# Seven block products planned by the whole PSUM bank in two phases, and other margins for choosing DVE

## The chip, the cores and the metric

The kernel runs on one core of a Trainium2 chip. The metric is the device time of one execution in microseconds, the median of several runs. The span of a profiled execution, from its first to its last instruction, is some 2 us (1.7 to 2.2) shorter than the time of the same execution. All runs told of here are in the fast state (granted TensorE clock 0.995 to 1.0). Runs of one call share a chip, and different calls may have had different chips: the kernel before had medians of 1513.98, 1514.43, 1515.01, 1515.30 and 1514.85 us in the five calls.

## The reference, cut to what matters

The input is 64 graphs of 256 nodes with 128 features, and one adjacency matrix `adj` (256 x 256) for all. Four graph layers follow one another; the change is in the first, a gated recurrence of five steps whose first product is with the adjacency matrix.

```python
def step(h, _):                                   # layer 0, five times
    m_in  = jnp.einsum('nm,bmd->bnd', in_matrix, h)    # in_matrix = out_matrix = adj
    m_out = jnp.einsum('nm,bmd->bnd', out_matrix, h)
    av = jnp.concatenate([m_in, m_out], axis=-1)
    u3 = h @ u3_w.T + u3_b
    z  = jax.nn.sigmoid(av @ w3_w.T + w3_b + u3)
    r  = jax.nn.sigmoid(av @ w4_w.T + w4_b + u3)
    hv = jnp.tanh(av @ w5_w.T + w5_b + (r * h @ u5_w.T + u5_b))
    h  = (1.0 - z) * h + z * hv
    ...                                            # layers 1 to 3 and the norms: cut
```

## The kernel before

The kernel treats two graphs at a time (32 pairs). It does not write its instructions in the order of the program text. A planner (`Schedule`) collects operations with the values that each reads and writes, the engines that could do it and a time for each, then lays them out one by one at the earliest start, and so fixes the order on every engine before the kernel runs. The parts that matter:

```python
SPARE = {"DVE": 0.6, "DVE+": 1.0, "POOL": 0.4}    # added to an option's end when an engine is chosen
MARGIN, LAG = 1.06, 0.8                           # LAG: margin between an operation and who waits for it
...
for engine, us, fn in op.ways:                    # choice of the engine (cut)
    start = max(op.ready, held, *(engines[e] for e in USES.get(engine, (engine,))))
    end = start + us + SPARE.get(engine, 0.0)
```

"DVE+" is a DVE operation with two SBUF operands, which the planner keeps apart from Pool's (both need what it calls PORT). The product with the adjacency matrix is done as seven 128x128 block products in place of eight (a Winograd form) in the five steps of 28 of the 32 pairs, so 140 times. They accumulate in three column parts (blocks of 128 columns) of one PSUM bank, and between them the partial sums are read out:

```python
def spread7(h, right, terms):
    sv, t, o = Value("A", name="sums"), Value("PS", name="ps"), Value("A", name="mT")
    X, Y, V = (Part(t) for _ in range(3))         # to the planner: three independent values
    ...
    product(0, H(0, 0), B(0, 0), [h], [X, Y, V], start=True)
    sum_(...)  sum_(...)  sum_(...)               # s1|s3, s2, s4: DVE or Pool
    copy(0, 0, [X], [o0])                         # ScalarE or DVE, 128 columns
    product(1, s1, T(0), [p1, V], [V])
    copy(3, 1, [V], [o3])
    product(2, H(0, 1), B(1, 0), [h, Y], [Y])
    plus(0, 2, [Y, o0], [o, o0])                  # DVE: PSUM + SBUF
    product(0, s2, T(1), [p2, X], [X])
    copy(1, 0, [X], [o1])
    product(1, s4, B(1, 1), [p4, V], [V])
    plus(1, 1, [V, o1], [o, o1])
    product(0, s3, T(2), [p1, X], [X])
    plus(3, 0, [X, o3], [o, o3])
    product(0, H(1, 1), T(3), [h, X], [X])
    copy(2, 0, [X], [o])
    return o
```

## Time and profile before

| | before |
|---|---|
| time, median (runs) | 1513.98 us (1513.24 to 1515.22, 4 runs) |
| TensorE, DVE, ScalarE, Pool busy | 99%, 79%, 66%, 41% |
| matmul records | 7156, of which 1960 are block products (line 565) |

TensorE is the engine to look at, and 99% is nearly all. But a busy TensorE in the profile includes modelled ends, which hide up to 0.17 us of every pause (two records of 128 columns are shown 0.39 us long and take 0.22 in a dense stream). So for this document I counted **gaps**. A gap is the distance from one matmul's start to the next, less what the first one takes in a dense stream (111.3 ns for 128 columns, 215.8 for 256, 429.2 for 512, as the traces show; 113.5 was taken for 130, where they show 111.8, which is 0.4 us in the whole sum; two records for each fp32 matmul), wherever that is over 25 ns. The dense stream is 1485.2 us long in both kernels. In the kernel before the gaps sum to 20.7 us, and 12.8 of them lie ahead of block products (L565 of the kernel before, the line of the helper that issues them). For the steady middle part of the span, 400 to 1300 us, they sum to 9.5 us. The windows view shows that part more coarsely; its columns are TensorE, weight loads, DVE, ScalarE and Pool busy, then clock, DMA share and GB/s:

```profile
400.00:1300.00 900.00, 895.51 (x4287) 628.89 (x4286) 724.28 (x1848) 606.30 (x1914) 393.53 (x515) 1.00 0.70 147
```

TensorE is without work for 4.5 us of 900 here; the other half of the 9.5 us is under modelled ends.

### The profile page before, as it was taken

What the parts mean: (1) busy time and instruction counts of PE and PEld (TensorE: products, weight loads), DVE (VectorE), ACT (ScalarE), POOL (GpSimd) and SP (SyncE); (2) the same over time, 40 slices, a digit from 0 to 9 for tenths busy, and PEclk for the clock granted to TensorE, in tenths of its full rate; (3) what the DMA queues carried; (4) which work ended last, traced back from release to release, by engine and by line L of the source; (5) the groups of instructions that cost most, each with busy time, mean ns of one, the idle gap of its engine ahead of it and who ended that gap; (6) DMA issues with size and microseconds to landing.
All of it is one profiled execution on the core that took longest, in us unless ns stands there. A gap on an engine that the chain in (4) does not pass through costs nothing.

```text
span 1513.6 us, 26330 instructions
## 1 busy us (share of the span) xinstructions
PE 1498.1 (99%) x7156; PEld 1060.8 (70%) x7156; DVE 1191.8 (79%) x3102; ACT 1006.1 (66%) x3173; POOL 626.9 (41%) x835
## 2 busy tenths in 40 slices
PE   9999999999999999999999999999999999999998
PEld 7556566767776677667676677676676666788987
DVE  7865778898889887888788878667878778789861
ACT  3444456787777676677666676665677567778974
POOL 5212233545455453445543454243444233335552
PEclk9999999999999999999999999999999999999999
DMA  6544456887888686677575776576676577678453
GB/s 195 131 82 93 98 127 137 166 174 161 171 177 171 130 163 152 135 152 163 125 162 125 157 166 132 124 153 134 128 159 133 122 157 156 124 164 173 96 120 77
DMA packets 936515, 214.39 MB, mean 142 GB/s; under 512 B 717744, under 2 KB 931888, under 8 KB 936368
## 3 DMA queue, kind: packets, MB, share of 16 engines
q1 hardware_dynamic: 936368, 212.71, 66.7%
q8 instruction: 58, 0.95, 0.3%
q14 instruction: 89, 0.73, 0.2%
HBM read 115.81 MB, written 96.80 MB: 140 GB/s over the span
## 4 chain that ended last, share of the span: by engine, by line
PE 94%; DVE 3%; ACT 1%; DMA 1%; issue 1%; SPq 0%; POOLq 0%; ACTq 0%; POOL 0%; DVEq 0%
PE ps L565 14%; PE ps L545 13%; PE ps L705 9%; PE ps L706 9%; PE ps L698 9%; PE ps L690 9%; PE ps L691 9%; PE ps L727 7%; PE ps L841 4%; PE ps L834 3%; PE ps L797 3%; PE ps L833 3%; PE ps L757 2%; DVE b L772 1%; DVE a L576 0%
## 5 line engine op out<-in xcount | busy, mean ns | idle before, releaser
L565 PEld LDWEIGHTS ps<-aTt,a 128*128 128x128 f32 x1064 | 165.5, 191 | 82.5 <-issue 56.3
L579 POOL TENSOR_TENSOR a<-a 128x256 f32<-128x256 f32 x100 | 83.0, 830 | 296.8 <-DMA a<-e 102.7
L576 DVE TENSOR_TENSOR a<-ps,a 128x128 f32<-128x128 f32 x420 | 109.6, 280 | 106.0 <-PE ps L565 84.9
L565 PE MATMUL ps<-aTt,a 128*128 128x128 f32 x1064 | 186.6, 276 | 5.1 <-DVE a L576 3.9
L708 ACT ACTIVATE a<-ps,bzrh 128x512 f32<-128x512 f32 x160 | 109.9, 687 | 109.6 <-PE ps L706 104.4
L572 ACT COPY a<-ps 128x128 f32<-128x128 f32 x489 | 117.4, 272 | 88.9 <-PE ps L565 70.1
L694 ACT ACTIVATE a<-ps,bzrh 128x512 f32<-128x512 f32 x160 | 110.0, 690 | 91.5 <-PE ps L691 74.3
L705 PE MATMUL ps<-a,w 128*128 128x512 f32 x320 | 163.6, 593 | 0.0
L706 PE MATMUL ps<-a,u5h 128*128 128x512 f32 x320 | 163.4, 592 | 0.0
L691 PE MATMUL ps<-a,w 128*128 128x512 f32 x320 | 163.4, 592 | 0.0
L698 PE MATMUL ps<-a,w 128*128 128x512 f32 x320 | 162.2, 593 | 0.0
L526 DVE STREAM_TRANSPOSE a<-a 128x512 f32<-128x512 f32 x217 | 151.1, 700 | 10.8 <-PE ps L706 2.2
L727 PEld LDWEIGHTS ps<-W,a 128*128 128x128 f32 x1024 | 135.6, 192 | 33.0 <-issue 29.2
L651 ACT ACTIVATE a<-ps 128x128 f32<-128x128 f32 x456 | 121.1, 287 | 48.2 <-PE ps L727 23.8
L659 POOL TENSOR_TENSOR s<-s,neg_half 128x4 f32<-128x4 f32 x128 | 144.4, 1128 | 9.3
L235 ACT COPY a<-ps 128x512 f32<-128x512 f32 (+1 forms) x164 | 85.2, 523 | 88.8 <-PE ps L545 59.6
L700 ACT ACTIVATE a<-ps,bzrh 128x512 f32<-128x512 f32 x160 | 109.7, 689 | 51.1 <-PE ps L698 42.3
L727 PE MATMUL ps<-W,a 128*128 128x128 f32 x1024 | 141.8, 275 | 0.0
L690 PE MATMUL ps<-a,W 128*128 128x512 f32 x256 | 131.1, 594 | 0.7 <-DVE x L673 0.7
L656 POOL TENSOR_SCALAR s<-s 128x4 f32<-128x4 f32 x96 | 30.0, 313 | 239.3 <-ACT a L651 199.4
L565 PEld LDWEIGHTS ps<-aT,a 128*128 128x128 f32 x728 | 108.4, 191 | 26.4 <-issue 20.8
L565 PE MATMUL ps<-aT,a 128*128 128x128 f32 x728 | 125.7, 276 | 0.6 <-issue 0.2
(199 smaller groups left out, 3367.9 us busy)
## 6 DMA issues: line engine op xcount, KB each, us to landing
e<-a SPq DMA_DIRECT2D x279, 256.0 KB
a<-e SPq DMA_DIRECT2D x1116, 64.0 KB
e<-b SPq DMA_DIRECT2D x29, 512.0 KB
b<-e SPq DMA_DIRECT2D x116, 128.0 KB
x<-x_in SPq DMA_DIRECT2D x32, 256.0 KB
t<-xT_in SPq DMA_DIRECT2D x32, 256.0 KB
a<-d SPq DMA_DIRECT2D x32, 256.0 KB
y_out<-a SPq DMA_DIRECT2D x32, 256.0 KB
```

The lines of the kernel that those rows point to most:

```text
L526: dve(n / 512 * 0.55 + 0.09, lambda: nc.vector.transpose(st.at(n), i.at(n)), [i], [st])
L545: nc.tensor.matmul(t.at(2, N)[:, b, :], tokens(i)[:, 2 * b + j, :], right.ap[:, j, :], start=(b == j == 0), stop=(j == 1), skip_group_chec ...
L565: pe(mm(128), lambda: nc.tensor.matmul(blk(t, k), left(), rt(), start=start, stop=True, skip_group_check=True), [*r, right, terms], w)
L572: S.add([("ACT", 0.18, lambda: nc.scalar.copy(blk(o, to), blk(t, k))), ("DVE", 0.2, lambda: nc.vector.tensor_copy(blk(o, to), blk(t, k)))] ...
L651: nc.scalar.activation(tokens(junk)[:, c, :], v.at(len(tiles), D)[:, k, :], AF.Square, scale=D ** -0.5, accum_out=mv()[:, c, 1:2])
L659: pool(1.02, lambda: nc.gpsimd.tensor_tensor(rs(), rs(), neg_half.ap, op=ALU.pow), [s, neg_half], [s])
L690: nc.tensor.matmul(t.at(512), mat("u3"), hT.at(512), start=True, stop=False)
L691: nc.tensor.matmul(t.at(512), w4.ap, mT.at(512), start=False, stop=True)
L698: pe(mm(512), lambda t=t, mT=mT: nc.tensor.matmul(t.at(512), w3.ap, mT.at(512), start=False, stop=True, skip_group_check=True), [w3, mT, t ...
L705: nc.tensor.matmul(t.at(512), w5.ap, mT.at(512), start=True, stop=False)
L706: nc.tensor.matmul(t.at(512), u5h.ap, r.at(512), start=False, stop=True)
L727: nc.tensor.matmul(tokens(t)[:, c, :], tokens(i)[:, c, :], w(), start=(first and k == c == 0), stop=(k == len(lefts) - 1), skip_group_chec ...
```

## The change

Its intent, as its title says: seven block products in two phases of one PSUM bank, with more room for DVE, each hand-over planned later, and two-operand sums preferred on Pool. The diff does the first of these. Its two SPARE numbers go down, and so make DVE more attractive to the planner than before, so for them I went by the diff and not by the words.

```diff
-SPARE = {"DVE": 0.6, "DVE+": 1.0, "POOL": 0.4}
+SPARE = {"DVE": 0.3, "DVE+": 0.6, "POOL": 0.4}
@@ spread7
-        sv, t, o = Value("A", name="sums"), Value("PS", name="ps"), Value("A", name="mT")
+        sv, o, t = Value("A", name="sums"), Value("A", name="mT"), bank()
-        X, Y, V = (Part(t) for _ in range(3))
-        o0, o1, o3 = (Part(o) for _ in range(3))
-        def product(k, left, rt, r, w, start=False):
-               [*r, right, terms], w)
+        def product(k, left, rt, r, start=False):
+               [*r, right, terms, *[t] * (not start)], [t])     # the whole bank
 ...                                   (the three sums stay; the old products and copies go)
+        product(0, H(0, 0), B(0, 0), [h], start=True)
+        product(1, s1, T(0), [p1])
+        product(3, s3, T(2), [p1])
+        product(2, s2, T(1), [p2])
+        evacuate(lambda: o.at(512), lambda: t.at(512), [t], [o])
+        sum_(0.335, 0.8, ... o[0:2] + o[2:4] ..., [o], [p1])
+        product(0, H(0, 1), B(1, 0), [h])
+        product(3, H(1, 1), T(3), [h])
+        product(1, s4, B(1, 1), [p4])
+        sum_(0.2, 0.46, ... blk(o, 3) ..., [p1], [o])
+        evacuate(lambda: blk(o, 0), lambda: blk(t, 0), [t], [o], (0.17, 0.2))
+        dve(0.335, ... tensor_add(o[1:3], t[1::2], sv[0]) ..., [t, p1], [o])
```

More of the change, by code (lines that the diff above doesn't have):

```diff
@@ L550, in spread7 @@
     def spread7(h, right, terms):
-        sv, t, o = Value("A", name="sums"), Value("PS", name="ps"), Value("A", name="mT")
+        sv, o, t = Value("A", name="sums"), Value("A", name="mT"), bank()
         p1, p2, p4 = (Part(sv) for _ in range(3))
-        X, Y, V = (Part(t) for _ in range(3))
-        o0, o1, o3 = (Part(o) for _ in range(3))
-        blk = lambda v, k, n=1: v.at(512)[:, k * P:(k + n) * P]
+        blk = lambda v, k: v.at(512)[:, k * P:(k + 1) * P]
         H = lambda b, j: lambda: blk(h, 2 * b + j)
@@ L562, in spread7 @@
         s3, s1, s2, s4 = (lambda k=k: blk(sv, k) for k in range(4))
-        def product(k, left, rt, r, w, start=False):
+        def product(k, left, rt, r, start=False):
             pe(mm(128), lambda: nc.tensor.matmul(blk(t, k), left(), rt(), start=start, stop=True, skip_group_check=True),
-               [*r, right, terms], w)
+               [*r, right, terms, *[t] * (not start)], [t])
         def sum_(us, us_pool, fn, r, w):
             S.add([("DVE+", us, lambda: fn(nc.vector)), ("POOL", us_pool, lambda: fn(nc.gpsimd))], r, w)
-        def copy(to, k, r, w):
-            S.add([("ACT", 0.18, lambda: nc.scalar.copy(blk(o, to), blk(t, k))),
-                   ("DVE", 0.2, lambda: nc.vector.tensor_copy(blk(o, to), blk(t, k)))], r, w)
-        def plus(to, k, r, w):
-            dve(0.2, lambda: nc.vector.tensor_add(blk(o, to), blk(t, k), blk(o, to)), r, w)
-        product(0, H(0, 0), B(0, 0), [h], [X, Y, V], start=True)
         sum_(0.335, 0.8, lambda e: e.tensor_sub(sv.at(4, P)[:, 0:2], h.at(4, P)[:, 0::2], h.at(4, P)[:, 2:4]), [h], [p1])
@@ L581, in spread7 @@
         sum_(0.2, 0.46, lambda e: e.tensor_add(s4(), s2(), H(0, 1)()), [h, p2], [p4])
-        copy(0, 0, [X], [o0])
-        product(1, s1, T(0), [p1, V], [V])
-        copy(3, 1, [V], [o3])
-        product(2, H(0, 1), B(1, 0), [h, Y], [Y])
-        plus(0, 2, [Y, o0], [o, o0])
-        product(0, s2, T(1), [p2, X], [X])
-        copy(1, 0, [X], [o1])
-        product(1, s4, B(1, 1), [p4, V], [V])
-        plus(1, 1, [V, o1], [o, o1])
-        product(0, s3, T(2), [p1, X], [X])
-        plus(3, 0, [X, o3], [o, o3])
-        product(0, H(1, 1), T(3), [h, X], [X])
-        copy(2, 0, [X], [o])
+        product(0, H(0, 0), B(0, 0), [h], start=True)
[3 more added lines that the diff above has]
+        evacuate(lambda: o.at(512), lambda: t.at(512), [t], [o])
+        sum_(0.335, 0.8, lambda e: e.tensor_add(sv.at(4, P)[:, 0:2], o.at(4, P)[:, 0:2], o.at(4, P)[:, 2:4]), [o], [p1])
+        product(0, H(0, 1), B(1, 0), [h])
+        product(3, H(1, 1), T(3), [h])
+        product(1, s4, B(1, 1), [p4])
+        sum_(0.2, 0.46, lambda e: e.tensor_add(blk(o, 3), blk(sv, 0), blk(sv, 1)), [p1], [o])
+        evacuate(lambda: blk(o, 0), lambda: blk(t, 0), [t], [o], (0.17, 0.2))
+        dve(0.335, lambda: nc.vector.tensor_add(o.at(4, P)[:, 1:3], t.at(4, P)[:, 1::2],
+                                                blk(sv, 0)[:, None, :].to_broadcast([P, 2, P])), [t, p1], [o])
         return o
```

## The prediction

> **What bounds the kernel now.** I read the page first, then the waits of TensorE, then windows of 100 us, then single stretches of the timeline. The page's engine totals and its chain of waits:
>
> ```profile
> PE 1498.1 (99%) x7156; PEld 1060.8 (70%) x7156; DVE 1191.8 (79%) x3102; ACT 1006.1 (66%) x3173; POOL 626.9 (41%) x835
> ...
> PE 94%; DVE 3%; ACT 1%; DMA 1%; issue 1%; SPq 0%; POOLq 0%; ACTq 0%; POOL 0%; DVEq 0%
> ```
>
> TensorE is busy nearly throughout and carries 94% of the chain that ends last. No other engine is a bound on average. What TensorE waited for, in full:
>
> ```profile
> PE ps L565 <- DVE a L576: 3.9, 9, 1.2
> PE ps L295 <- DVE ones L293: 1.2, 1, 1.2
> PE ps L545 <- DMA a<-e: 1.2, 1, 1.2
> PE ps L565 <- ACT a L572: 1.0, 3, 0.6
> PE ps L690 <- DVE x L673: 0.7, 1, 0.7
> ```
>
> L565 is the helper that issues the seven block products, L572/L573 their copies out of PSUM, L576 the PSUM additions. So the changed part is the one that TensorE visibly waits in, but for 5 us of 1513.6 only.
>
> "Busy" uses modelled ends, so I also count starts. The groups by shape hold about 3,820 matmul records of 128 (or 130) columns, 1,720 of 256 and 1,600 of 512 (every fp32 product shows as two records). Inside a burst the timeline gives 0.111 us per 128-column record, 0.216 per 256 and 0.43 per 512:
>
> ```profile
> 508.22 0.61 PE L565 MATMUL ps<-aTt,a 128*128 128x128 f32 x4
> 508.66 0.61 PE L565 MATMUL ps<-aT,a 128*128 128x128 f32 x4
> 509.11 0.39 PE L565 MATMUL ps<-aTt,a 128*128 128x128 f32 x2
> 509.33 0.39 PE L565 MATMUL ps<-aT,a 128*128 128x128 f32 x2
> 509.55 0.60 PE L833 MATMUL ps<-vx,a 128*128 128x256 f32 x2
> 509.99 0.59 PE L834 MATMUL ps<-vq,a 128*128 128x256 f32 x2
> ```
>
> (508.22 to 508.66 is four records of 128, 509.55 to 509.99 two of 256.) The sum is 3820 x 0.111 + 1720 x 0.216 + 1600 x 0.43 = 424 + 372 + 688 = 1484 us. With 1.2 us before the first matmul and 6.1 after the last (1513.6 less 1507.5), the matmuls alone need 1491 us. **All the slack there is comes to about 22 us, 1.5% of the span**, and part of it is start-up and the last pairs, which the change does not touch.
>
> DVE is the second engine, and in places it is much closer to its limit than 79%:
>
> ```profile
> 300.00:400.00 100.00, 99.60 (x493) 69.90 (x492) 90.00 (x252) 78.97 (x264) 45.12 (x62) 1.00 0.81 170
> 400.00:500.00 100.00, 99.59 (x490) 70.90 (x489) 88.40 (x228) 71.10 (x225) 49.82 (x62) 1.00 0.82 171
> 500.00:600.00 100.00, 98.55 (x499) 71.36 (x498) 80.66 (x202) 66.54 (x222) 47.24 (x64) 1.00 0.70 144
> ```
>
> (columns: TensorE, weight loads, DVE, ACT, Pool busy). At DVE 90% TensorE still lost only 0.4 us of 100.
>
> [...] this is how the longest visible TensorE wait arose:
>
> ```profile
> 509.78 1.45 POOL L803 TENSOR_TENSOR a<-a,rbc 128x512 f32<-128x512 f32 x1
> ```
>
> ```profile
> 510.03 1.48 DVE L772 CUSTOM_DVE_ANT_0 b<-a,maskb 128x256 f32<-128x256 f32 x1
> ...
> 512.87 1.14 DVE L696 SCALAR_TENSOR_TENSOR a<-a,t 128x512 f32<-128x512 f32 x1
> 513.93 0.47 DVE L576 TENSOR_TENSOR a<-ps,a 128x128 f32<-128x128 f32 x2
> ```
>
> The L772 operation (median 0.42 us) took 1.48 until Pool's ended; another was stretched behind the next Pool sum; L576 came late, and the product at 514.55 waited 1.17 us for it.
>
> [...] Here the 128x256 sum (L579) has a median of 0.73 us on Pool and 0.416 on DVE, 1.76 times.
>
> [...] The kernel before orders a step's products and evacuations by column part of one bank; the kernel after orders them by the whole bank. No row of the trace before shows a collision or its cost, so I put no time on this.
>
> **The change part by part.** The block products are used in 28 of the 32 pairs, in 5 steps: 140 calls.
>
> TensorE: seven products before, seven after. Still 140 x 7 x 2 = 1960 records. No matmul time is removed.
>
> Hand-overs: before, block 0 of the bank is written, read and rewritten three times, so TensorE waits on an evacuation up to five times a call (V, Y, X parts). After, four products are issued, one evacuation follows, then three products: one hand-over. With the planner's own constants block 0's old chain is about four products (0.22+1.03 each, with its margin for the semaphore) and four reads (0.2+0.96): 9.6 us; the new one 4 products, a 0.5 us evacuation, 3 products, a 0.35 us addition: about 5.5. A bank is thus held shorter, and a step ends some 3 to 4 us sooner. Since many pairs are in flight, this is latency which TensorE already covers. It can give back at most part of the visible 5.7 us at L565 and the tails of the same gaps hidden by modelled ends; I take half of 10: **minus 5 us**.
>
> PSUM readers per call: out go four 128-column copies (560 in all: 489 ACT at 0.272, 71 DVE at 0.283) and three additions (420 at 0.280 = 110 us of DVE). In come a 512-column and a 128-column evacuation (mostly ACT, 0.59 and 0.27) and one 128x256 addition from PSUM (0.41, from the L673 rows: 57 us of DVE). ACT: minus 133, plus about 140 x 0.86 x 0.85 = 102: 30 us less. DVE: minus 110 minus 20 plus 57 plus about 20: **53 us less**.
>
> SBUF sums per call: three before, five after (two more: one of 256 columns, one of 128). Which engine gets them is set by the SPARE numbers, an amount added to an option's planned end. I compare the options at equal starting time. The 256-column sum before: DVE 0.335 x 1.06 + 1.0 = 1.355 against Pool 0.8 x 1.06 + 0.4 = 1.248, so Pool by 0.11; the trace has 125 on Pool, 15 on DVE. After: DVE 0.955 against 1.248, DVE by 0.29. The 128-column sum before: Pool by 0.32 (254 of 280 on Pool); after: 0.812 against 0.888, DVE by 0.08. So whatever the title says of Pool, these numbers favour DVE more than before. As a guide, an option that DVE won by 0.10 before (the two-operand additions of 512) went to DVE two times in three (L803: 20 of 32). I take 75% of 280 sums of 256 and 62% of 420 of 128: 210 x 0.416 + 260 x 0.28 = 160 us on DVE against 14 now. Some 35 of the 65 512-column sums now on Pool move as well: 25 us. The lower plain DVE margin (0.6 to 0.3) draws some evacuations and normalisations from ACT: 15 us. **DVE plus 186 less 53: plus about 130 us at most, 88% of the span**. The planner itself sees a full DVE and then sends to Pool, so I expect about half: 1220 to 1290. Pool stays near 600, ACT near 950.
>
> What this costs: in the stretch where DVE is at 88-90% it would go to about 93-95%, and a plan whose DVE operations run a few per cent over their planned time falls behind the 0.8 us of margin more often. I have no row that prices it. Estimate: three to four waits of about 1 us more per 100 us over the stretch from 200 to 500, and one per 100 in the rest: **plus 9 us**. Sum: 1514 - 5 + 9 = 1518.
>
> **The rivals.**
> (a) Pure relief: fewer hand-overs, fewer PSUM operations and fewer Pool operations [...], so DVE's stretched operations shrink. For it: [...] the 420 small additions gone. Against it: hardly anything to win. Time 1503 to 1510.
> (b) DVE becomes the bound in the middle: the sums pile on it in the first third, and TensorE waits at the tanh and gate products (L690, L706), not at L565. For it: 90% in a window already, and the lower SPARE. Against it: TensorE lost nothing at 90%. Time 1530 to 1560.
> (c) Re-ordering alone: any edit reshuffles the whole static order, the last pairs too, where TensorE loses most (57.2 busy of the last 64 us). Either way by some 6 us.
> (d) The new whole-bank hand-over takes the place of the old ones: phase two must wait for the evacuation. The planner puts other products between, so I expect little.
>
> **Range and chances.** Floor 1491 and an unreachable zero of waits make a gain above 2% (below 1484) impossible without fewer matmuls: 0.01, left for surprises. A loss above 2% (beyond 1544) needs TensorE's idle time to triple, rival (b) in full: 0.06. Predicted 1518, range 1507 to 1535; within 2%: 0.93.
>
> **What would show it.** L565 still 1960 records and TensorE busy within 5 us of 1498; the DVE share up to 81-85%, ACT down by 30 to 60 us; Pool within 60 of 627; more than half of the two-operand sums on DVE; TensorE's waits on the block helper fewer, and waits on DVE in gate lines more. Wrong if DVE's busy time falls (then the relief of (a) wins and the time is below 1512), or if the windows from 200 to 500 lose over 3 us of TensorE each (then (b)).

## The result, and the profile after

The kernel after takes 1501.49 us (1500.96 to 1502.10, 4 runs) against 1513.98 (4 runs). The ratio is 0.9917, with a 95% interval of 0.9900 to 0.9934. Ratios here are the mean time of one kernel's fast runs over that of the other's of the same rounds, so not quite the ratio of the medians quoted. It is 12.5 us faster; I had predicted 4 us slower, and 1501.49 is below my range of 1507 to 1535. By the rule of 2% it counts as the same.

The page of the kernel after, engine totals and the chain that ended last:

```profile
PE 1490.5 (99%) x7156; PEld 1061.3 (71%) x7156; DVE 1266.0 (84%) x3250; ACT 972.0 (65%) x2802; POOL 562.9 (38%) x743
...
PE 99%; ACT 0%; issue 0%; POOLq 0%; DVE 0%; ACTq 0%; POOL 0%
```

The matmul records are as many as before, DVE works 74 us more, and TensorE now makes up 99% of the chain instead of 94%. Everything that TensorE visibly waited for:

```profile
PE ps L718 <- ACT ps L235: 2.1, 1, 2.1
PE ps L295 <- DVE ones L293: 1.2, 1, 1.2
```

One wait of the start-up is left, and one in the last pairs (L718). The block helper, now L563, isn't in the list: before, it had 3.9 us on DVE and 1.0 on ScalarE. The windows:

```profile
300.00:400.00 100.00, 100.00 (x465) 67.81 (x465) 96.32 (x247) 72.14 (x195) 48.45 (x61) 1.00 0.79 166
400.00:500.00 100.00, 100.00 (x507) 72.18 (x506) 85.49 (x223) 65.32 (x197) 39.57 (x57) 1.00 0.76 156
500.00:600.00 100.00, 100.00 (x492) 71.12 (x491) 87.44 (x224) 65.91 (x201) 39.06 (x52) 1.00 0.72 152
```

```profile
400.00:1300.00 900.00, 900.00 (x4315) 634.62 (x4314) 769.31 (x1913) 593.28 (x1715) 343.90 (x452) 1.00 0.70 146
```

At a DVE share of 96% TensorE lost nothing. The gaps sum to 7.0 us, of which 0.0 lie between 400 and 1300 us and 0.1 ahead of block products. The account closes: 20.7 less 7.0 is 13.7 us, and the two spans differ by 1513.6 - 1500.0 = 13.6.

### The profile page after: what moved, and what is told of

Read it like the earlier page. It is cut to its first block, busy times and chain, and to the rows that moved or that the text cites. A ratio compares the mean times of both kernels' runs of the same rounds, so it can differ in the third digit from the quotient of the medians.

```text
span 1500.0 us, 26032 instructions
## 1 busy us (share of the span) xinstructions
PE 1490.5 (99%) x7156; PEld 1061.3 (71%) x7156; DVE 1266.0 (84%) x3250; ACT 972.0 (65%) x2802; POOL 562.9 (38%) x743
## 4 chain that ended last, share of the span: by engine, by line
PE 99%; ACT 0%; issue 0%; POOLq 0%; DVE 0%; ACTq 0%; POOL 0%
PE ps L563 15%; PE ps L545 13%; PE ps L689 9%; PE ps L696 9%; PE ps L681 9%; PE ps L682 9%; PE ps L697 9%; PE ps L718 8%; PE ps L788 4%; PE ps L824 4%; PE ps L832 4%; PE ps L825 4%; PE ps L748 2%; PE ps L520 0%; PE ps L295 0%; PE ps L456 0%
## 5 line engine op out<-in xcount | busy, mean ns | idle before, releaser
L235 ACT COPY a<-ps 128x512 f32<-128x512 f32 (+2 forms) x434 | 192.5, 459 | 148.4 <-PE ps L545 75.4
L563 PEld LDWEIGHTS ps<-aTt,a 128*128 128x128 f32 x1064 | 157.9, 192 | 40.7 <-issue 36.6
L563 PE MATMUL ps<-aTt,a 128*128 128x128 f32 x1064 | 179.4, 275 | 0.0
L718 PEld LDWEIGHTS ps<-W,a 128*128 128x128 f32 x1024 | 138.5, 193 | 34.9 <-issue 28.9
L563 PEld LDWEIGHTS ps<-aT,a 128*128 128x128 f32 x728 | 118.9, 191 | 61.2 <-issue 50.9
L718 PE MATMUL ps<-W,a 128*128 128x128 f32 x1024 | 148.6, 276 | 2.1 <-ACT ps L235 2.1
L563 PE MATMUL ps<-aT,a 128*128 128x128 f32 x728 | 135.0, 274 | 0.0
L578 POOL TENSOR_TENSOR a<-a 128x256 f32<-128x256 f32 x49 | 43.9, 898 | 225.4 <-ACT a L235 223.9
L701 DVE TENSOR_TENSOR a<-a,a 128x512 f32<-128x512 f32 x128 | 91.8, 718 | 34.0 <-ACT a L699 33.8
L702 DVE SCALAR_TENSOR_TENSOR a<-a,a 128x512 f32<-128x512 f32 x160 | 113.1, 708 | 7.8 <-ACT a L691 6.3
L697 PEld LDWEIGHTS ps<-a,u5h 128*128 128x128 f32 x320 | 60.8, 190 | 76.5 <-issue 65.5
```

Source lines behind the costliest of these rows:

```text
L235: S.add([("ACT", us[0], lambda: nc.scalar.copy(o(), i())), ("DVE", us[1], lambda: nc.vector.tensor_copy(o(), i()))], r, w)
L563: pe(mm(128), lambda: nc.tensor.matmul(blk(t, k), left(), rt(), start=start, stop=True, skip_group_check=True), [*r, right, terms, *[t] * ...
L697: nc.tensor.matmul(t.at(512), u5h.ap, r.at(512), start=False, stop=True)
L718: nc.tensor.matmul(tokens(t)[:, c, :], tokens(i)[:, c, :], w(), start=(first and k == c == 0), stop=(k == len(lefts) - 1), skip_group_chec ...
```

## The experiments

The time went out of TensorE's pauses. The question is which part of the change removed them. The theories were these.

- **A**, fewer hand-overs: a call hands the bank back to TensorE once, no longer up to five times. (A hand-over is a read of the bank by ScalarE or DVE that stands between two products of one call.)
- **B**, the routing: new SPARE numbers, so fewer Pool operations beside which DVE's run long. (In the trace of the kernel before, DVE's 128 operations of L772 took at most 0.425 us in the 49 cases where Pool's overlapped them by no more than 50 ns; the 79 others took 0.58 us on average and up to 1.53.)
- **C**, chance: any edit reshuffles the whole static order.
- **H**, formed after the eighth run: the planner of the kernel before did not know of waits that the built program contains, because it took parts of one bank for independent values.

Fifteen kernels ran, all timed in three rounds, each beside the kernel before of its own call. The gap columns are worked out from each run's profiled execution, as above.

| kernel | median us | ratio to before (95%) | gaps, all | gaps, 400 to 1300 us | gaps ahead of the block products |
|---|---|---|---|---|---|
| before | 1513.98 | | 20.7 | 9.5 | 12.8 |
| after | 1501.49 | 0.9917 (0.9900 to 0.9934) | 7.0 | 0.0 | 0.1 |
| spare_only | 1517.83 | 1.0025 (1.0017 to 1.0034) | 23.8 | 10.1 | 14.7 |
| form_only | 1500.75 | 0.9908 (0.9891 to 0.9925) | 6.2 | 0.0 | 0.6 |
| before_lag11 | 1526.82 | 1.0075 (1.0060 to 1.0090) | 29.6 | 9.5 | 21.0 |
| before_due31 | 1511.74 | 0.9982 (0.9974 to 0.9989) | 16.9 | 5.9 | 9.9 |
| after_due31 | 1502.39 | 0.9919 (0.9904 to 0.9934) | 7.0 | 0.0 | 0.1 |
| after_evac_dve | 1504.28 | 0.9933 (0.9918 to 0.9948) | 9.3 | 0.0 | 2.3 |
| before_two_banks (wrong result) | 1518.68 | 1.0024 (1.0014 to 1.0035) | 24.7 | 12.4 | 14.4 |
| before_whole6 (wrong result) | 1540.22 | 1.0166 (1.0149 to 1.0183) | 45.0 | 13.7 | 29.9 |
| before_whole3 | 1510.28 | 0.9963 (0.9948 to 0.9978) | 15.6 | 1.5 | 7.8 |
| before_whole3_rr | 1509.32 | 0.9963 (0.9948 to 0.9977) | 13.5 | 0.2 | 7.4 |
| after_four_whole | 1502.33 | 0.9912 (0.9898 to 0.9927) | 8.6 | 0.5 | 0.6 |
| after_four_parts | 1513.35 | 0.9987 (0.9980 to 0.9993) | 18.1 | 8.6 | 13.0 |
| after_l3 | 1502.37 | 0.9921 (0.9905 to 0.9938) | 12.3 | 0.4 | 1.5 |
| form_l3b | 1502.80 | 0.9919 (0.9904 to 0.9934) | 11.0 | 0.0 | 1.0 |
| after_l3b | 1499.99 | 0.9903 (0.9887 to 0.9920) | 7.1 | 0.0 | 0.1 |

### The two halves of the change: spare_only and form_only

```diff
 # spare_only: the kernel before with
-SPARE = {"DVE": 0.6, "DVE+": 1.0, "POOL": 0.4}
+SPARE = {"DVE": 0.3, "DVE+": 0.6, "POOL": 0.4}
 # form_only: the kernel after with that line turned back
```

> The block products of the kernel before with the new SPARE numbers alone. Theory A (the form: one hand-over a call instead of up to five takes TensorE's waits at the block helper away): those waits stay, the gaps ahead of L565 stay near 13 us, time 1508 to 1518. Rival B (the routing: more sums on DVE, fewer Pool operations [...], takes them away): gaps ahead of L565 under 4 us, time 1499 to 1504.

> The new two-phase form with the old SPARE numbers. Theory A: gaps ahead of the block helper stay under 2 us, time 1499 to 1505. Rival B: the waits come back, time 1508 to 1515, with more of the five sums on Pool (over 60%).

The form alone gives the whole gain (1500.75 us), and the numbers alone cost 0.25%. The page of form_only also speaks against B's mechanism:

```profile
PE 1490.3 (99%) x7156; PEld 1059.8 (71%) x7156; DVE 1173.3 (78%) x2832; ACT 999.7 (67%) x2901; POOL 826.3 (55%) x1097
```

Pool is busy for 826 us here, 200 more than before, so there are more operations beside which DVE's can run long, and still TensorE has no gap in the middle (0.0 us). In spare_only Pool falls to 474 us, and the waits on L576 stay:

```profile
PE ps L565 <- DVE a L576: 4.6, 11, 1.1
PE ps L565 <- ACT a L572: 1.4, 3, 0.9
```

B falls. In the stretch that my prediction showed, one addition did come late, after DVE operations that took 1.48 and 1.14 us beside Pool's (medians 0.42 and 0.68). But what makes such a delay cost TensorE time is something in the old form: 12.8 us of gaps lie ahead of its block products, and 0.6 in form_only.

### Chance: before_due31 and after_due31

```diff
-DUE, LAST_DUE, LAST = 30.0, 9.0, 8
+DUE, LAST_DUE, LAST = 31.0, 9.0, 8
```

> The kernel before with one number of the planner's priorities changed from 30 to 31, which reshuffles the order and should mean nothing: it measures chance (rival C). If the gain of 12.5 us is chance of the order, this should move by as much, 5 us or more; if not, it stays at 1511 to 1517.

> The kernel after with the meaningless change of one priority number from 30 to 31: the same control for chance as was run on the kernel before. Expected 1499 to 1504, gaps ahead of the helper under 1 us. If chance makes the gain, it moves by 5 us or more.

The shuffle moves the kernel before by 0.18% (2.7 us) and leaves the kernel after at 1502.39. The gap ahead of the block products stays large in the one (9.9 us) and absent in the other (0.1). As far as one shuffle of each kernel shows, C makes up to 2 to 3 us of a difference, not 12.

### More margin in the old form: before_lag11

```diff
-MARGIN, LAG = 1.06, 0.8
+MARGIN, LAG = 1.06, 1.1
```

> The kernel before with the planner's margin for every hand-over raised from 0.8 to 1.1 us. If the waits at L565 are hand-overs that come a little later than planned (theory A's mechanism), the gaps ahead of L565 fall from 13 to under 7 us and the time to 1503 to 1509, unless the longer plan holds tiles so long that TensorE is left without work elsewhere. [...] the margin removes fewer than half: 1508 to 1514.

It became slower, by 0.75%, which is outside both expectations (1503 to 1509 us for A's mechanism; 1508 to 1514 for B's, by which the margin removes fewer than half of the gaps). The gaps in the middle are 9.5 us, just as before; what grew are those of the first 400 us (16.3 us in place of 8.2), so the longer plan cost time at the start. The margin that the planner puts between an operation and those waiting for it doesn't reach the waits of the middle, although it was made for that. Under A, in the way I had put it (hand-overs a little later than planned), it should have helped. This was the first hint, no more, that the waits aren't in the plan at all.

### Which engine hands back: after_evac_dve

```diff
-        evacuate(lambda: o.at(512), lambda: t.at(512), [t], [o])
+        dve(0.61, lambda: nc.vector.tensor_copy(o.at(512), t.at(512)), [t], [o])
```

> The kernel after, with the one 512-column evacuation between the phases always on DVE instead of mostly on ScalarE; still one hand-over a call. If the number of hand-overs per call is what counts (A1), gaps ahead of the block helper stay under 2 us and the time between 1500 and 1506. If it counts which engine hands back (A2: DVE is late, [...] ScalarE is not), they come back to 4 us or more and the time is above 1506. DVE's load rises by about 75 us either way.

This took 1504.28 us, and the helper's 2.3 us of gaps are one wait of 1.5 us for a sum and smaller ones at the first and last products. None lies at the hand-over between the phases, although 120 of the 140 calls there now wait for DVE in the built program (the list of instructions that the kernel makes, with the engines that each waits for). One planned hand-over through DVE a call cost TensorE nothing at that place.

### No hand-over within a call: before_two_banks

```diff
-        X, Y, V = (Part(t) for _ in range(3))
+        K = [Part(t) for _ in range(4)] + [Part(u) for _ in range(3)]     # u: a second bank
 ...  (each of the seven products to a block of its own; the same seven readers)
```

> The products, copies and additions of the kernel before, but spread over seven blocks of two PSUM banks, so that no product waits for an evacuation of its own call; old SPARE numbers. If the hand-overs back to TensorE within a call cause the waits (A), gaps ahead of the helper fall from 13 to under 4 us and the time to 1500 to 1507, though more small PSUM operations run than in the kernel after. If the small ScalarE and DVE operations themselves cause them (they make those engines late for everything), gaps stay above 8 us and the time above 1509. A shortage of banks would show as gaps at other lines.

I had overlooked that the products accumulate in their block on purpose, so the result is wrong; the instructions and waits are still those of the idea. A expected the gaps to go. They stayed: 12.4 us in the middle and 14.4 ahead of the helper. The list of instructions built from this kernel showed why. It names the engines that each instruction waits for, and products whose own block nobody had read still waited for ScalarE or DVE. In this program TensorE takes turns with ScalarE and DVE on a PSUM bank, by the bank and not by the block. In its trace 14.3 of the 14.4 us lie ahead of the 207 products that follow a reader of another block and none of their own.

So theory H: with X, Y and V as independent values the planner lays a product of one block beside a copy of another. The built program does not do that. One of the two waits, nothing in the plan has left room for it, and where it is the product, TensorE pauses (one such pause, of 0.35 us, is shown in the next section). The form after names the whole bank in every read and write, so that its plan and its program agree.

### The test of H in the new form: after_four_whole and after_four_parts

Both cut the evacuation between the phases into four copies of 128 columns. They differ in what the planner is told only; the engines and the order that it then chooses differ too.

```diff
 # both
-        evacuate(lambda: o.at(512), lambda: t.at(512), [t], [o])
+        for k in range(4):
+            evacuate(lambda k=k: blk(o, k), lambda k=k: blk(t, k), [t], [o], (0.18, 0.2))
 # after_four_parts also
+        K = [Part(t) for _ in range(4)]
-               [*r, right, terms, *[t] * (not start)], [t])
+               [*r, right, terms, *[K[k]] * (not start)], K if start else [K[k]])
 ...  (the copies and the last addition read K[k] in place of t)
```

> The kernel after with the evacuation between the phases cut into four 128-column copies, the planner still told the whole bank. It separates the number of small PSUM operations from the planning. H: gaps ahead of the helper stay under 1.5 us, time 1499 to 1505. If small operations make the engines late: gaps above 4 us, time above 1506.

> The converse of H: the same four copies in the kernel after, but the planner told column parts, as the kernel before does it, so that it may plan a product of one block beside a copy of another. H: the waits come back, gaps ahead of the helper 5 us or more, time 1505 to 1515. Theory A: one hand-over a block as in after_four_whole, so gaps and time as there, within 2 us.

This is the cleanest pair: 1502.33 us when told the bank, 1513.35 when told parts; gaps ahead of the helper 0.6 and 13.0 us. The waits of TensorE on that line, first told the bank, then parts:

```profile
PE ps L563 <- ACT a L235: 0.2, 1, 0.2
```

```profile
PE ps L564 <- ACT a L235: 6.5, 18, 0.5
```

And the middle windows in the same order:

```profile
400.00:1300.00 900.00, 899.78 (x4322) 634.53 (x4321) 791.03 (x2017) 582.50 (x1898) 304.39 (x410) 1.00 0.71 148
```

```profile
400.00:1300.00 900.00, 895.50 (x4284) 629.07 (x4283) 766.96 (x1970) 592.14 (x1909) 310.69 (x426) 1.00 0.70 146
```

The four small copies alone cost nothing that shows, but the planning by parts costs 4.3 us of busy time (8.1 us of gaps) in this stretch. In the built programs the second to fourth product of a call, which need only sums of DVE or Pool, wait for ScalarE 76 times in 420 when planned by parts, and never when planned by the bank. This is one such wait in the timeline of after_four_parts (start, length, engine and line, and in brackets the idle time and who ended it):

```profile
560.25 0.39 PE L564 MATMUL ps<-aTt,a 128*128 128x128 f32 x2
...
560.67 0.27 ACT L235 COPY a<-ps 128x128 f32<-128x128 f32 x1 [0.31 <-PE ps L564]
...
560.99 0.71 PE L564 MATMUL ps<-aTt,a 128*128 128x128 f32 x4 [0.35 <-ACT a L235]
```

By the built program, three blocks of one bank are at work here. The product at 560.25 is the second of its call and writes block 1. The copy at 560.67 reads block 0, and yet starts only when that product is done. The product at 560.99 is the third of the call and writes block 3, and yet waits for that copy.

A last check needs no new run. The traces hold two records for each of the 980 products, in the order of the built program, so each gap can be put to its product. The table sorts the products by which blocks ScalarE or DVE read between a product and the one before it in its call (number of products: us of gaps ahead of them).

| kernel | blocks of other products only | its own and others | its own only | no reader, or first in its bank |
|---|---|---|---|---|
| before | 136: 4.1 | 224: 7.9 | 113: 0.2 | 507: 0.6 |
| before_two_banks | 207: 14.3 | 0 | 0 | 773: 0.1 |
| after_four_parts | 136: 11.3 | 107: 1.4 | 5: 0.0 | 732: 0.4 |
| after_four_whole | 0 | 140: 0.5 | 0 | 840: 0.1 |

Where the planner was told parts, nearly all the gaps lie ahead of products that follow a reader of another block, which is the wait it did not know of. Products of the kernel before that follow a reader of their own block alone, which it did know of, have 0.2 us. The pair differs in the count of hand-overs too (1.8 a call in after_four_parts, 1.0 in after_four_whole), but the added gaps lie at the unplanned ones.

### The test of H in the old form: before_whole6, before_whole3, before_whole3_rr

```diff
 # all: the planner is told the bank
-               [*r, right, terms], w)
+               [*r, right, terms, *[t] * (not start)], [t])
 # whole6: the order of the text kept (product, read, product, read, ...)
 # whole3: products 0, 1, 2 | their three reads | two products | two reads | product | read | product | read
 # whole3_rr: as whole3, and every read also "writes" t, so that reads follow one another too
-        copy(0, 0, [t], [o0])
+        copy(0, 0, [t], [t, o0])
```

> New theory H, after the two-bank run: the built program makes TensorE, DVE and ScalarE wait for one another on any two accesses of one PSUM bank, but the planner of the kernel before believes the column parts X, Y, V independent, so it plans without these waits and leaves no margin for them. Here the products, copies and additions of the kernel before are kept, but the planner is told the whole bank for each, in strict alternation: six hand-overs a call, more than before. H: gaps ahead of L565 fall from 13 to under 3 us in spite of that, time 1500 to 1507. Theory A (count of hand-overs): gaps stay or grow, 10 us or more, time 1511 or more.

> As before_whole6, but with the products grouped so that three hand-overs a call remain, about as many as the longest part had in the kernel before; planner told the whole bank. H: gaps ahead of the helper under 3 us, time 1500 to 1506. Theory A: about as before, gaps 8 us or more.

> As before_whole3, with the planner also told that two reads of the bank by different engines follow one another (every access of the bank exclusive). If the 7.8 us of gaps that stayed in before_whole3 were reads of ScalarE and DVE waiting for each other unplanned (H extended to reads), gaps ahead of the helper fall under 3 us and the time to 1500 to 1507. If they come from handing back through DVE three times a call, whatever is planned, they stay at 6 us or more and the time at 1508 or more.

The first of these is a miss. With six hand-overs in strict sequence it took 1540.22 us, with gaps of 29.9 us ahead of the helper, where H as I had written it expected under 3. Its result was also wrong (relative error 0.09). The kernel, built again and simulated without a chip, differs from the kernel before in one of the 64 graphs only (relative error 0.087), and its plan hands a buffer to pair 15 about 0.6 us before its last reader, in pair 27, has started. That slip of the planner touches one buffer, so the time still counts, and it counts against H in its first wording: all six hand-overs are in the plan, and 13.7 us of gaps lie in the middle. To be in the plan is not enough when products and readers alternate strictly. That such a sequence has no other work to put into the pauses is possible, but not shown.

With three hand-overs the result is right. By the numbers of the whole run, both kernels miss what H expected: before_whole3 has 7.8 us of gaps ahead of the helper, close to the 8 of theory A, and before_whole3_rr with 7.4 us and 1509.32 us falls on the other side of its expectation. But the steady part does what H says: the gaps between 400 and 1300 us fall from 9.5 us to 1.5, and to 0.2 when the reads are planned in sequence too. The windows of before_whole3_rr:

```profile
0.00:400.00 400.00, 394.19 (x1733) 255.50 (x1734) 314.52 (x754) 230.91 (x660) 152.51 (x212) 1.00 0.64 139
400.00:1300.00 900.00, 900.00 (x4310) 634.70 (x4309) 705.53 (x1785) 623.20 (x2000) 390.86 (x515) 1.00 0.70 146
1300.00:1507.00 207.00, 198.68 (x1117) 170.03 (x1115) 151.86 (x496) 158.95 (x578) 97.96 (x126) 0.99 0.63 133
```

These are the old operations, with three hand-overs and three DVE additions a call, and TensorE shows no pause in 900 us. The built program of the kernel before has 3.4 hand-overs a call (473 in 140 calls), nearly as many. So it was not their number (A) that cost time there, though before_whole6 suggests that six a call do. But the time falls only to 1509.32 us, and 7.4 us of gaps ahead of the helper stay, all of them in the first 400 us. There the kernel before loses less (396.89 us busy, 4.4 us of such gaps), and the kernel after does better still:

```profile
0.00:400.00 400.00, 398.80 (x1769) 260.57 (x1770) 351.10 (x854) 234.92 (x570) 129.22 (x173) 1.00 0.66 143
```

TensorE pauses for 1.2 us of the first 400 in place of 5.8 in before_whole3_rr. In this stretch a single hand-over a call may count, as A says; no run separates it. Whether reads need to be planned in sequence as well isn't settled by the times (1510.28 and 1509.32 us, both 0.9963 of before).

### A version that might beat both: after_l3, form_l3b, after_l3b

The new helper costs TensorE 14 x 0.111 = 1.56 us where the plain product costs 8 x 0.216 = 1.73, and in the kernel after it brings only 0.1 us of gaps. The last layer has such a product too.

```diff
-        qT = to_sbuf(spread(x3, aT), "qT")
+        qT = spread7(x3, aT, aTt) if p < n_pairs - FINAL else to_sbuf(spread(x3, aT), "qT")   # after_l3
+        qT = spread7(x3, aT, aTt) if 4 <= p < n_pairs - 10 else ...                           # the other two
```

> A try at a better version: the kernel after with the same helper also for the adjacency product of the last layer in 30 pairs. A call takes 14 matmul records of 0.111 us in place of 8 of 0.216, 1.56 us against 1.73, so TensorE's floor falls by 30 x 0.17 = 5 us, and DVE and ScalarE get about 1 us more a call. If the new form keeps TensorE free of waits, 1494 to 1499; if DVE's load brings waits, 1500 to 1508.

> A try at a better version: the new form with the old SPARE numbers, and the helper also in the last layer of pairs 4 to 21 (18 pairs), away from the start and from the last pairs where the wider use lost 6 us. Floor 18 x 0.17 = 3.1 us lower; 1496.5 to 1499.5 if no waits are added, 1501 or more if they are.

> The same with the new SPARE numbers: 1497 to 1500 if no waits are added.

Used in 30 pairs it lost in the last pairs what it won: the dense stream is 5.0 us shorter, but the gaps are 5.3 us more, 6.4 of them in all between 1300 and 1400 us. Kept away from the start and the end it gave 1499.99 us with the new SPARE numbers and 1502.80 with the old. The profile of after_l3b agrees with the arithmetic (stream 3.0 us shorter, gaps 7.1 us as in the kernel after, span 1497.1 in place of 1500.0). But after_l3b and the kernel after were not timed in the same call, and the intervals of their ratios overlap, so it may be better by 1 to 3 us, which is not shown.

## Why the prediction was wrong

**What held.** The bound is TensorE, no matmul was removed (1064 + 728 + 112 + 56 = 1960 block records in both), and a gain above 2% was out of reach. My floor of 1484 us for the dense stream is 1485.2 by the fuller count. DVE went to 1266 us, within my 1220 to 1290, and to 84% (81 to 85%); ScalarE fell by 34 us (30 to 60); Pool fell by 64, just outside my 60. 417 of the 700 two-operand sums of the block products (60%) went to DVE, more than half as I had said. The sizes of the work were right.

**The step that failed first** is the one on PSUM. I wrote that the kernel before orders accesses "by column part of one bank" and the kernel after "by the whole bank", that no row of the trace "shows a collision or its cost", "so I put no time on this". That was the cause of most of the loss. The sign to look for wasn't a collision but a wait: a product waiting for a reader of another block. The pair after_four_whole and after_four_parts prices it at 12.4 us of gaps ahead of the helper and 11 us of time; in the kernel before, 12.0 of the 12.8 us lie ahead of products that follow a reader of another block.

**The term "minus 5 us"** for the hand-overs was too small for the same reason. I took half of 10 us, because I reckoned the latency of hand-overs to be covered with many pairs in flight. For up to three planned hand-overs a call that is right in the middle (after_evac_dve and before_whole3_rr have 0.0 and 0.2 us of gaps there). For waits that aren't planned it is not, and 12.6 us came back (12.76 to 0.13). On the same ground rival (d), that the new whole-bank hand-over would take the place of the old ones, is false, as I expected.

**The term "plus 9 us"** for DVE's load was wrong outright. I had in my own lines a window with DVE at 90% where TensorE lost 0.4 us of 100, and still priced 93 to 95% at three to four waits per 100 us, with, as I wrote, "no row that prices it". The sum was wrong as well: at about 1 us a wait, those rates make 9 to 12 us from 200 to 500 us and some 12 in the rest, 21 to 24 and not 9. In the kernel after, DVE reached 96% between 300 and 400 us at no loss. The new SPARE numbers cost 0.25% in the old form and nothing that shows in the new one (1501.49 against 1500.75 us, in different calls).

**Smaller slips**, which move no conclusion: 420 additions at 0.280 us are 118 us, and 110 is the busy time of a group whose records overlap. The new chain of "about 5.5" leaves out the 0.96 us of its last read, which the old chain of 9.6 counts; like for like it is 6.4.

**The rival that came nearest** is (a), pure relief, 1503 to 1510, which I held back because there was "hardly anything to win". There were 22 us of slack by my own floor, and 13.7 of them were won. My sentence that a falling DVE time would be the sign of (a) was false too: DVE's time rose, and relief came all the same. So was its third reason, fewer Pool operations: form_only has 200 us more of them and the same relief.

**What stays open.** Told the bank (and regrouped, so not purely by being told), the old operations win back 20.7 - 13.5 = 7.2 us of gaps: 9.3 us in the middle, less 2.1 us lost elsewhere. The other 6.5 us, to the kernel after, lie outside the middle but for 0.2. That the shorter call with a single hand-over does this, when few pairs are in flight, fits A and the windows, but no run separates it. Nor is it shown why TensorE pauses in before_whole6, where all hand-overs are planned.

## What to carry to other kernels

A plan must name what the program will really wait for: if the program takes turns on a whole bank, model the bank, even when the data of its parts are independent (1502.33 us planned by the bank, 1513.35 by parts). Finer parts in the model look like freedom and turned here into waits for which no margin was left (13.0 us of gaps ahead of the helper, against 0.6), and more margin for every hand-over did not help them (0.75% slower). Naming the bank is not enough alone: group the products too, since six planned hand-overs a call were worse than the old form (1540.22 us, 1.7% slower). And an engine at 90% and more beside the bound need not cost anything, as DVE at 96% didn't here (TensorE was busy for 100.00 of those 100 us): look for the bound's gaps by start times before pricing another engine's load.
